# Third-layer units of a four-layer graph attention kernel: elementwise work from VectorE to GpSimd

## The chip, the core and the metric

The kernel runs on one core of one Trainium2 chip. The core has TensorE (PE), VectorE (DVE), ScalarE (ACT), GpSimd (POOL) and SyncE (SP), which work side by side, each through its own instructions in order. The metric is the device time of one execution in microseconds (us). Before the change the median of four runs is 1438.87 us (1433.23 to 1440.81).

## What is computed

Eight batches of 2048 nodes with 64 features pass through four layers over the same 2048x2048 0/1 matrix `adj`. Layers 0 to 2 are graph attention: every pair of nodes has a score, a softmax over the neighbours, and a weighted sum of features. Every layer ends with a residual and a layer normalization. Layer 3, the one that the change is about, has a softmax per feature:

```python
# after layer 2
x = _layernorm(x + _L2_gnn_ref(x, adj, ...), axis=-1)
# layer 3
feat = softplus(x * (INV_SQRT2 * w0) + b0)
scores = feat * wa + ba
attn = softmax(where(adj > 0, scores[j], -1e9), axis=j)   # per i and feature d
out = einsum('bijd,bjd->bid', attn, feat)
x = _layernorm(x + out, axis=-1)
```

Since the scores of layer 3 depend on j and d only, the kernel writes it as two products with the mask: numerator = mask @ (feat * exp(scores)), denominator = mask @ exp(scores), and divides.

## The kernel before

**Units.** `todo` lists 24 attention units (layer, batch): layers 0 and 1 in two halves of four batches, then layer 2 for batches 0 to 7. Below, (2,b) is the layer-2 unit of batch b. A unit runs over sixteen blocks jb of 128 neighbours. `weights` (line 920) makes a 128x2048 tile w on VectorE: the maximum of a row r and a column, times the mask. `exponential` (930) is done by ScalarE, and `products` (969) by TensorE, which sums four 512-wide products per block in PSUM. `reach` (949) emits the weights of layer 2 up to two blocks ahead of the products and the exponentials up to one ahead. The row r of layer 2 lies in PSUM; one buffer serves all units, and `spread` (767) has TensorE write the next unit's row over it once the last weights of a unit have read it.

**What runs beside a unit.** Python generators in `Streams` (1294) are stepped once per block (`bg.step()`), and every `yield` is a step. So the order of the instructions on each engine is written by the program, and the class `InOrder` (70) keeps it: every compute instruction goes through its line 80, which is why the profile gives nearly all of them as L80 and groups are told apart by the names of tiles.

**After a layer-2 unit** a chain of two generators runs during the next unit:
- `finish` (988): ScalarE copies the sums, TensorE transposes them (p_o), VectorE divides (den, o), adds the residual, and `stats` (508) gives sums, the sum of squares (sq_x) and, through GpSimd's power of -0.5 in `inv_std` (492, line 503), the two columns rs and nm. Line 506 has VectorE compute nm after the power. Then lines 1074 and 1075 normalize the rows: o * rs, and that + nm into x. The first needs only rs, the second nm too.
- `l3_features` (1109), one step later: SP stores x to HBM (1124), and `softplus` (381) follows: ScalarE's Abs and Exp, a step later Ln and Relu with two loads of its function table around them, a step later the sum f + y (389). In the step of that sum GpSimd computes the scores d in two instructions (1129, 1130) and VectorE reduces f over the nodes (fs, 1132). Two steps later ScalarE takes exp(d), one more step later comes the numerator f * d (1137).
- For the products both numerator and exponentials are split in two pieces: ScalarE copies the first (v, 1164), and the second is the difference (1168), four 128x512 instructions per batch. In the code before, the first batch of a pair (i = 0) has them on GpSimd and the second on VectorE. Batch 6 waits at line 1142 until the last unit is over.

**Layer 3's products** (`l3_products`, 1207) start when a pair of batches has both its pieces. TensorE multiplies 16x2 pieces with a block of the mask, half a block (16 products) per step, in between the attention products. The mask arrives in quarters by SP's queue (`fetch`, 1197, issued at 1202), five buffers ahead; after the last unit ScalarE and GpSimd make it by turns (`widen`, 1180). `l3_finish` (1259) then takes the reciprocal on VectorE, the product with the numerator, the residual and the second normalization on GpSimd while units still run, and the stores at line 1288.

**The phase.** `now[0]` is the layer of the running unit, 0 to 2, and becomes 3 at line 1424, when the loop over units is over and only the background streams go on. `l3_finish` already chooses its engine by it (`pool if now[0] < 3 else dve`, lines 1276 and 1284).

Of the kernel before, what the change touches and what calls it, by code (L numbers as in the profile page):

```python
# [15 lines left out]
ALU = mybir.AluOpType  # L16
# [34 lines left out]
def gnn4_kernel(ctx: ExitStack, tc: tile.TileContext, t, out):  # L51
# [55 lines left out]
    class Banks:  # L107
# [4 lines left out]
        pool = None  # L112
# [28 lines left out]
    pe, dve, act, pool = (InOrder(e) for e in (nc.tensor, nc.vector, nc.scalar, nc.gpsimd))  # L141
# [4 lines left out]
    def bc_f(v, n=K, f=F):  # L146
        return v[:, :, None].to_broadcast([P, n, f])

    def bc_k(v, n=K, f=F):
        return v[:, None, :].to_broadcast([P, n, f])  # L150
# [65 lines left out]
    src = t["L0_gnn_a"]  # L216
# [161 lines left out]
    nc.gpsimd.memset(ext[:, 1:2], -X_MAX)  # L378
    fext = consts.tile([P, 2], F32, name="fext")

    def softplus(f, y, src):

        act.activation(y, src, AF.Abs, scale=l3c[:, 0:1], bias=l3c[:, 1:2])
        act.activation(y, y, AF.Exp, scale=-1.0)
        yield 1
        act.activation(y, y, AF.Ln, bias=1.0)
        act.activation(f, src, AF.Relu, scale=l3c[:, 0:1], bias=l3c[:, 1:2])
        yield 1
        dve.tensor_tensor(f, f, y, ALU.add)

    rs_w, last_w, a_cols = [], [], [None]
    for layer in range(3):
        rs = early.tile([P, F1], F32, tag="rs_w", name=f"rs_{layer}")
# [594 lines left out]
    def finish(u):  # L988
        layer, b = u.layer, u.b
        yield from oT_slots.take()  # L990
        oT = tmp.tile([P, 2, 512], F32, tag="oT", name=f"oT_{u.n}")
        for c in range(2):
            act.copy(oT[:, c], u.acc[c])
        if layer == 0:
            hb = early.tile([P, K, F], F32, tag="hb", name=f"hb_{u.n}", bufs=1)
            for sl, y in V[0, b].parts:
                pool.tensor_tensor(
                    hb[:, :, sl], y, bc_k(gamma[:, sl], K, y.shape[2]), ALU.mult
                )
        yield 1  # L1000
        yield from o_slots.take()
        o = tmp.tile([P, K, F], F32, tag="o", name=f"o_{u.n}", bufs=2)
        o5 = o.rearrange("p (c h s) f -> p c s h f", c=2, h=2)
        done = 0
        while done < 4:
            width = Banks.width()
            ps = []
            yield from pm_slots.take(width)
            for i in range(done, min(done + width, 4)):
                c, s0 = i // 2, 2 * (i % 2)  # L1010
                p = psum(f"p_o_{u.n}_{c}_{s0}")
                for s in range(2):
                    k = s0 + s
                    pe.matmul(
                        p[:, s * 2 * F1 : (s + 1) * 2 * F1],
                        lhsT=oT[:, c, k * P : (k + 1) * P],
                        rhs=RH[layer].rearrange("p h f -> p (h f)"),
                        start=True,
                        stop=True,
                    )  # L1020
                ps.append((c, s0, p))
            done += width
            if done >= 4:
                oT_slots.give()
            yield 2 if width == 2 else 1
            for c, s0, p in ps:
                p4 = p[:, : 4 * F1].rearrange("p (s h f) -> p s h f", s=2, h=2)
                den = small.tile([P, 2, 2], F32, tag="den", name=f"den_{u.n}_{c}_{s0}")
                dve.reciprocal(den, p4[:, :, :, F])
                if layer == 2:  # L1030
                    dve.tensor_tensor(
                        o5[:, c, s0 : s0 + 2],
                        p4[:, :, :, :F],
                        den[:, :, :, None].to_broadcast([P, 2, 2, F]),
                        ALU.mult,
                    )
                    continue
                for s in range(2):
                    for h in range(2):
                        act.activation(  # L1040
                            o5[:, c, s0 + s, h],
                            p4[:, s, h, :F],
                            AF.Copy,
                            scale=den[:, s, h : h + 1],
                        )
            pm_slots.give(width)
        if layer == 2:
            for sl, x in x_cur[b].parts:
                dve.scalar_tensor_tensor(o[:, :, sl], o[:, :, sl], 0.0, x, ALU.max, ALU.add)
            yield 1  # L1050
        else:
            yield 1
            if layer == 0:
                pool.tensor_tensor(o, o, hb, ALU.add)
                yield 2

            yield from e_slots.take()
            e = tmp.tile([P, K, F], F32, tag="e", name=f"eh_{u.n}")
            act.activation(e, o, AF.Relu, scale=-1.0)
            act.activation(e, e, AF.Exp, scale=-1.0)  # L1060
            yield 1
            for sl, x in x_cur[b].parts:
                pool.tensor_tensor(
                    e[:, :, sl], e[:, :, sl], x, ALU.add
                )
            act.activation(o, o, AF.Relu)
            yield 1
            pool.tensor_tensor(o, o, e, ALU.add)
            e_slots.give()
            yield 2  # L1070
        nm, rs = yield from stats(o, K, f"x_{u.n}")
        xn = Rows(x_cur[b].t, layer < 2)
        if layer == 2:
            dve.tensor_tensor(o, o, bc_f(rs), ALU.mult)
            dve.tensor_tensor(xn.v, o, bc_f(nm), ALU.add)
        else:
            yield 1
            for k in range(K):
                act.activation(
                    xn.block(k), o[:, k], AF.Identity, scale=rs[:, k : k + 1], bias=nm[:, k : k + 1]  # L1080
                )
                if k % 4 == 3:
                    yield 1
            xn.settle()
        o_slots.give()
        x_cur[b] = xn
        V[layer + 1, b] = xn
        if layer < 2:
            yield 1
# [7 lines left out]
    now = [0, 0, 0]  # L1097
# [11 lines left out]
    def l3_features(b):  # L1109

        if b % 2 == 0:
            q = Pair()
            q.bs, q.n, q.fm, q.x, q.ready = [b, b + 1], f"{b}", {}, {}, 0
            pairs.append(q)
        else:
            q = pairs[-1]
        i = b % 2
        n = f"3_{b}"
        slots, tag = ((h_slots, "h"), (xT_slots, "xT"))[i]
        yield from slots.take()  # L1120
        yield from e_slots.take()
        f = x_cur[b].v
        q.x[i] = dram.tile([P, K, F], F32, tag="x3_d", name=f"x3_d_{b}", bufs=B)
        nc.sync.dma_start(q.x[i], f)
        y = tmp.tile([P, K, F], F32, tag="e", name=f"sp_{n}")
        yield from softplus(f, y, f)
        e_slots.give()
        d = tmp.tile([P, K, F], F32, tag=tag, name=f"d_{n}")
        pool.tensor_tensor(d, f, bc_k(wa), ALU.mult)
        pool.tensor_tensor(d, d, bc_k(l3off), ALU.add)  # L1130
        fs = small.tile([P, F], F32, tag="fs", name=f"fs_{n}")
        dve.tensor_reduce(fs, f.rearrange("p k f -> p f k"), AX.X, ALU.add)
        bg.add(l3_mean(q, i, fs, n))
        yield 2
        act.activation(d, d, AF.Exp)
        yield 1
        dve.tensor_tensor(f, f, d, ALU.mult)
        yield 1

        if i == 0:  # L1140
            if b == B - 2:
                while now[0] < 3:
                    yield 1
            else:
                yield from v_slots.take()
            q.v = [
                [
                    (work if b == B - 2 else late).tile(
                        [P, K2, 2, 2, F],
                        F32R,  # L1150
                        tag="w" if b == B - 2 else f"v{m}{h}",
                        name=f"v{m}_{h}_{q.n}",
                        bufs=4 if b == B - 2 else 1,
                    )
                    for h in range(2)
                ]
                for m in range(2)
            ]
        else:
            while not hasattr(q, "v"):  # L1160
                yield 1
        parts = [(h, w, (f, d)[w][:, h * K2 : (h + 1) * K2]) for h in range(2) for w in range(2)]
        for h, w, src in parts:
            act.copy(q.v[0][h][:, :, i, w], src)
        yield 1
        eng = dve if i else pool
        for h, w, src in parts:
            eng.tensor_tensor(
                q.v[1][h][:, :, i, w], src, q.v[0][h][:, :, i, w].bitcast(F32), ALU.subtract
            )  # L1170
        slots.give()
        yield 1
        q.ready += 1
# [759 lines left out]
```

## Time and profile before

| | |
|---|---|
| median of the runs | 1438.87 us |
| the profiled execution's own time | 1438.47 us |
| its span in the trace | 1436.7 us |
| last attention product (end of the units) | 1285.5 us |
| mean granted TensorE clock | 0.947 of full speed |

The span is what the trace covers, from the first instruction to the last; the execution's own time has 1.8 us around it. The page has the busy time of each engine, then the span in 40 equal slices of some 36 us whose digits are busy tenths. The layer-2 units take the 23rd to the 36th slice or so; what follows is layer 3 alone. Rows of an engine in order of time have start, duration, engine, operation and tiles, and in brackets the idle time before and what ended it.

### The profile page before, as it was taken

The page shows a single profiled execution, that of the slowest core. Times are in us where ns is not written, and L with a number is a line of the kernel's source. Part 1 is how long each engine was busy: PE and PEld are TensorE (multiplying, and loading weights), DVE is VectorE, ACT ScalarE, POOL GpSimd, SP SyncE. Part 2 cuts the span into 40 slices and gives each one's busy share as a digit, 9 for nine tenths or more (in the row PEclk, how much of TensorE's full clock was granted, in tenths as well). Part 3 has the DMA queues.
Part 4 walks back from the last instruction along what each step waited for, and adds up shares of the span by engine and source line. Part 5 has one row for each costly group of instructions (what it writes and reads, how often), then busy time and mean ns, then how long its engine had stood idle before and what let it go on. Part 6 is the DMA issues. An engine that isn't in the chain of part 4 may idle for free.

```text
span 1436.7 us, 19117 instructions
## 1 busy us (share of the span) xinstructions
PE 1235.9 (86%) x7138; PEld 620.6 (43%) x7138; DVE 1259.9 (88%) x1260; ACT 820.5 (57%) x1585; POOL 549.9 (38%) x619
## 2 busy tenths in 40 slices
PE   3679788988899988999998887879999898978896
PEld 2323233333233333344332332336565564648896
DVE  4699889997899999899999898898989989878876
ACT  4415444664557545555533986787677767574442
POOL 1152463324423344332322211312445535367665
PEclk9989999999999999999999897999999999999998
DMA  8730000000000022221201000005453354431111
GB/s 303 247 77 1 1 2 1 1 2 1 2 1 1 25 65 88 89 75 56 66 16 37 1 1 15 15 24 150 130 153 100 110 152 128 134 108 34 34 38 33
DMA packets 113335, 90.36 MB, mean 63 GB/s; under 512 B 58077, under 2 KB 91021, under 8 KB 112082
## 3 DMA queue, kind: packets, MB, share of 16 engines
q1 hardware_dynamic: 112690, 87.89, 20.4%
q8 instruction: 58, 0.95, 0.3%
q10 hardware_dynamic: 544, 1.17, 0.2%
q14 instruction: 43, 0.35, 0.1%
HBM read 63.54 MB, written 25.46 MB: 62 GB/s over the span
## 4 chain that ended last, share of the span: by engine, by line
PE 30%; DVE 19%; ACT 8%; issue 4%; POOL 2%; DMA 1%; SPq 0%; DVEq 0%; POOLq 0%; ACTq 0%
PE p_l L80 14%; PE acc L80 13%; DVE w L80 12%; ACT w L80 3%; DVE st_x L80 2%; ACT x L80 2%; PE p_o L80 1%; DVE o L80 1%; ACT sp L80 1%; DMA mask<-mask_d 1%; PE r L80 1%; POOL o L80 1%; DVE x L80 1%; DVE fs L80 1%; POOL st_x L80 1%
## 5 line engine op out<-in xcount | busy, mean ns | idle before, releaser
L80 DVE SCALAR_TENSOR_TENSOR w<-r,se,edge 128x2048 f32<-128x2048 f32 (+1 forms) x270 | 555.5, 2103 | 22.8 <-PE r L80 20.0
L80 PE MATMUL acc<-w,pv 128*64 128x512 f32 x2048 | 508.7, 629 | 71.0 <-DVE w L80 64.0
L80 DVE SCALAR_TENSOR_TENSOR w<-r,lo_g,edge 128x2048 f32<-128x2048 f32 (+1 forms) x144 | 298.0, 2096 | 18.0 <-PE r L80 9.7
L80 PE MATMUL acc<-w,x 128*64 128x512 f32 x1024 | 266.4, 651 | 38.6 <-ACT w L80 34.5
L80 ACT ACTIVATE w<-w,down_g 128x2048 f32<-128x2048 f32 (+1 forms) x144 | 257.4, 1809 | 70.5 <-DVE w L80 70.0
L80 PEld LDWEIGHTS p_l<-v,mask 128*128 128x128 f32 x2048 | 253.7, 194 | 66.1 <-issue 49.4
L80 PE MATMUL p_l<-v,mask 128*128 128x256 f32 x2048 | 269.7, 289 | 11.8 <-POOL mask L80 6.3
L80 PEld LDWEIGHTS acc<-w,pv 128*64 128x64 f32 x2048 | 133.3, 141 | 338.2 <-issue 190.4
L80 PEld LDWEIGHTS acc<-w,x 128*64 128x64 f32 x1024 | 67.8, 145 | 163.9 <-issue 91.4
L80 ACT COPY oT<-acc 128x512 f32<-128x512 f32 x48 | 25.8, 589 | 144.4 <-PE acc L80 144.4
L80 ACT ACTIVATE x<-o,st_x 128x64 f32<-128x64 f32 x256 | 90.6, 446 | 3.4 <-DVE st_x L80 3.4
L80 ACT ACTIVATE o<-p_o,den 128x64 f32<-128x64 f32 x256 | 55.9, 327 | 44.6 <-DVE den L80 44.6
L80 ACT ACTIVATE nd<-p_l,empty 128x256 f32<-128x256 f32 x64 | 30.2, 472 | 88.4 <-PE p_l L80 88.4
L80 POOL TENSOR_SCALAR isw_x<-isw_x 128x16 f32<-128x16 f32 x24 | 6.3, 262 | 181.3 <-DVE isw_x L80 169.8
L80 POOL TENSOR_TENSOR st_x<-isw_x,mhalf 128x16 f32<-128x16 f32 x24 | 70.4, 2931 | 2.0
L80 PEld LDWEIGHTS p_o<-rh,oT 128*128 128x128 f32 x384 | 49.7, 196 | 35.9 <-issue 15.4
L80 POOL TENSOR_TENSOR st_h<-isw_h,mhalf 128x16 f32<-128x16 f32 x8 | 23.6, 2953 | 106.4 <-DVE isw_h L80 83.5
L80 PE MATMUL p_o<-rh,oT 128*128 128x130 f32 x384 | 59.9, 293 | 4.6 <-ACT o L80 3.6
L80 DVE RECIPROCAL nd<-nd 128x256 f32<-128x256 f32 x32 | 55.8, 1743 | 0.0
L80 POOL TENSOR_TENSOR eh<-eh,x 128x1024 f32<-128x1024 f32 (+2 forms) x24 | 36.5, 1533 | 45.3 <-ACT eh L80 45.2
L80 POOL COPY x<-x 128x16 f32<-128x16 f32 x16 | 3.3, 206 | 123.8 <-ACT x L80 123.8
L80 DVE SCALAR_TENSOR_TENSOR w<-row,se,edge 128x2048 f32<-128x2048 f32 x16 | 39.6, 2485 | 10.0 <-DMA row<-row_d 10.0
(243 smaller groups left out, 1486.5 us busy)
## 6 DMA issues: line engine op xcount, KB each, us to landing
mask<-mask_d SPq DMA_DIRECT2D x140, 256.0 KB
mask_d<-mf SPq DMA_DIRECT2D x32, 512.0 KB
raw<-in_adjT_dram SPq DMA_DIRECT2D x8, 1024.0 KB
raw<-in_adjT_dram SPq DMA_DIRECT2D x16, 512.0 KB
x<-in_x_dram SPq DMA_DIRECT2D x8, 512.0 KB
x_d<-x SPq DMA_DIRECT2D x8, 512.0 KB
e<-x_d SPq DMA_DIRECT2D x64, 64.0 KB
out_dram<-o SPq DMA_DIRECT2D x64, 64.0 KB
```

Source lines behind the costliest of these rows:

```text
L80: ins = f(*args, **kwargs)
```

## The change

Four places take their engine from the phase: normalization of layer 2, sum of softplus, numerator, and second pieces run on GpSimd while units run and on VectorE after. The engine of the second pieces no longer depends on the place i of the batch in its pair. The call of softplus for two constants at the start keeps VectorE. No instruction is added or left out, and no `yield` moves.

```diff
-    def softplus(f, y, src):
+    def softplus(f, y, src, eng=dve):
...
-        dve.tensor_tensor(f, f, y, ALU.add)
+        eng.tensor_tensor(f, f, y, ALU.add)
...
         if layer == 2:
-            dve.tensor_tensor(o, o, bc_f(rs), ALU.mult)
-            dve.tensor_tensor(xn.v, o, bc_f(nm), ALU.add)
+            side = pool if now[0] < 3 else dve
+            side.tensor_tensor(o, o, bc_f(rs), ALU.mult)
+            side.tensor_tensor(xn.v, o, bc_f(nm), ALU.add)
...
-        yield from softplus(f, y, f)
+        side = pool if now[0] < 3 else dve
+        yield from softplus(f, y, f, side)
...
-        dve.tensor_tensor(f, f, d, ALU.mult)
+        side = pool if now[0] < 3 else dve
+        side.tensor_tensor(f, f, d, ALU.mult)
...
-        eng = dve if i else pool
+        eng = pool if now[0] < 3 else dve
         for h, w, src in parts:
             eng.tensor_tensor(
                 q.v[1][h][:, :, i, w], src, q.v[0][h][:, :, i, w].bitcast(F32), ALU.subtract
             )
```

## The prediction

> **What bounds the kernel now.** I read the page first, then the table by stretch with one row per attention unit of layer 2, then the chain of waits, then each engine in order of time where a moved instruction stands. I write (2,b) for the time in which batch b's unit ends on TensorE; the third-layer work of batch b-1 runs beside it.
>
> ```profile
> PE 1235.9 (86%) x7138; PEld 620.6 (43%) x7138; DVE 1259.9 (88%) x1260; ACT 820.5 (57%) x1585; POOL 549.9 (38%) x619
> ...
> PE   3679788988899988999998887879999898978896
> ...
> DVE  4699889997899999899999898898989989878876
> ACT  4415444664557545555533986787677767574442
> POOL 1152463324423344332322211312445535367665
> ```
>
> VectorE has the largest share (88%), GpSimd the smallest (38%), so the page suggests a gain. But the share is an average; the units are what counts:
>
> ```profile
> core 0: us, PE busy (x) PEld busy (x) DVE busy (x) ACT busy (x) POOL busy (x), PEclk, DMA share, GB/s
> ...
> 835.70:896.30 60.60, 47.62 (x249) 17.62 (x250) 54.66 (x65) 46.32 (x46) 8.44 (x7) 0.83 0.02 9
> 896.30:951.50 55.20, 43.89 (x351) 16.92 (x347) 48.20 (x44) 44.16 (x34) 16.50 (x13) 0.88 0.04 14
> 951.50:1012.80 61.30, 58.76 (x346) 33.91 (x346) 56.17 (x51) 45.28 (x37) 14.90 (x17) 1.00 0.38 114
> 1012.80:1079.00 66.20, 64.78 (x396) 39.57 (x393) 58.76 (x61) 46.15 (x40) 28.02 (x35) 1.00 0.51 143
> 1079.00:1147.90 68.90, 61.08 (x354) 34.83 (x350) 63.95 (x69) 49.06 (x45) 36.52 (x43) 0.98 0.35 100
> 1147.90:1217.00 69.10, 64.50 (x379) 38.36 (x378) 62.92 (x63) 46.86 (x39) 29.87 (x37) 0.98 0.47 141
> 1217.00:1285.50 68.50, 62.25 (x363) 36.10 (x359) 56.70 (x61) 46.33 (x43) 31.69 (x39) 0.95 0.40 118
> ```
>
> In (2,1) and (2,2) TensorE idles 24.3 us and VectorE leads. From (2,3) on the third layer's products stand between the attention products and TensorE is almost full: 22.6 us idle in 334 us. A faster VectorE can take no more than these 47 us, and in the last five units only where TensorE waits for it. After 1285.5 the code keeps VectorE.
>
> **What moves.** The condition is read when an instruction is emitted, so I count by place. Normalization: seven batches, two instructions each (batch 7's follow the last unit). Sum of softplus: seven. Numerator: six; batch 6's (at 1287.95) follows the exponential that ScalarE does after the last unit's first copies, at least one step later, so it stays. Second pieces: batches 1, 3, 5 (four each) go to GpSimd, and batch 6's four go the other way, because they are always emitted after the last unit.
>
> ```profile
> L80 DVE TENSOR_TENSOR x<-o,st_x 128x1024 f32<-128x1024 f32 x8 | 11.2, 1404 | 0.3
> L80 DVE TENSOR_TENSOR x<-x,sp 128x1024 f32<-128x1024 f32 x8 | 9.8, 1225 | 11.4 <-ACT x L80 11.4
> L80 DVE TENSOR_TENSOR x<-x,d 128x1024 f32<-128x1024 f32 x8 | 9.7, 1217 | 5.3 <-ACT d L80 5.3
> ```
>
> ```profile
> L80 POOL TENSOR_TENSOR d<-d,l3off 128x1024 f32<-128x1024 f32 x8 | 19.2, 2405 | 0.6
> ```
>
> VectorE loses 7 x (1.21 + 1.40) + 7 x 1.23 + 6 x 1.22 + 12.8 (the twelve pieces, contended ones included) - 4 x 0.68 = 44 us of work. GpSimd's row for the same shape is 2.40 us (2.38 to 2.44 undisturbed) and its pieces take 1.28, so it gains 27 x 2.40 + 12 x 1.28 - 4 x 1.28 = 75 us; at 28 to 37 of 69 us per unit it has room. The price is latency: +2.4 us for a normalization, +1.2 for a sum.
>
> **The wait that is added.** Behind the softplus sum VectorE has nothing but the reduction of its result, in the same step:
>
> ```profile
> 1196.28 1.23 DVE L80 TENSOR_TENSOR x<-x,sp 128x1024 f32<-128x1024 f32 x1 [1.07 <-ACT x L80]
> 1197.55 2.05 DVE L80 TENSOR_REDUCE fs<-x 128x64 f32<-128x1024 f32 x1
> 1199.51 2.35 DVE L80 SCALAR_TENSOR_TENSOR w<-r,lo_g,edge 128x2048 f32<-128x2048 f32 x1
> 1201.76 0.74 DVE L80 SCALAR_TENSOR_TENSOR st<-st 128x4 f32<-128x4 f32 x1
> ```
>
> VectorE is in order and already waited 1.07 us for ScalarE here. Now it waits 2.40 us instead of working 1.23, so its queue moves back by 1.2, not forward. Queued behind are the weights w. And ScalarE's Abs, at the head of the softplus, waits for the slower normalization; Exp, Ln, Relu and the exponentials of w queue behind it. Who waits for that is in TensorE's order: the row r of the next unit overwrites what the last weights read.
>
> ```profile
> 1206.52 1.28 PE L80 MATMUL r<-row,ones 3*128 3x512 bf16 x4 [4.11 <-DVE w L80]
> ```
>
> **Unit by unit**, by the starts in the rows:
> - (2,1): GpSimd's power ends at 860.55 and the first half of the normalization needs only that; VectorE's small st_x instruction is held until it ends (863.2), the second half ends at 865.8. Abs starts there instead of 864.57; Relu ends 1.2 later, the sum 2.4 instead of 1.2 after it. The 2.4 us that VectorE wins before turn into idle. The row r, for which TensorE stood 3.54 us, comes later: +1.8 us.
> - (2,2): GpSimd must first finish its amT pieces (to about 927.3 without contention), the normalization ends at 932.2, Abs 3.0 late, reduction 4.2 late, r 4.2 late. Numerator (1.1) and pieces (2.4) leave VectorE afterwards, but ScalarE's copies follow TensorE's end, so they pay back 0.6: +3.6 us.
> - (2,3): sum behind the last weights, TensorE full: 0. (2,4): same; the product o<-nd no longer collides with the normalization, TensorE's 0.75 us wait for the mask behind it in SP's queue goes: -0.7.
> - (2,5): the pieces held VectorE 4.58 us. TensorE's waits from 1112 to 1141 (0.81, 0.85, 1.80, 1.56, 0.71, sum 5.7) partly go; GpSimd needs 8 x 1.28 = 10.2 us, ready for the first product at 1112.49. Small two-input instructions now wait for it, ScalarE's table loads stay: between -1.6 and -3.4, I take -2.5.
> - (2,6): GpSimd reaches the normalization at 1185.2 (behind o<-o,e), ends at 1190.0; Abs 2.5 late, the reduction 3.6 late, r at 1210.2: +3.7.
> - (2,7): ScalarE's casts bound it; sum behind the last weights: 0.
> - Tail: the sum on GpSimd delays its out rows by 1.1, SP's queue holds mask fetches behind their transfers, TensorE waits for those at 1292.57: +1.1. Batch 6's pieces (2.7 us) fit into VectorE's 3.5 us idle before 1296.6; without that cover they cost up to 2.7.
>
> TensorE works at half pace after long waits (3.68 us for eight products at 940.26, 1.94 at 933.45). Longer waits in (2,2) and (2,6) may cost 0 to 1.8 each; I take 1.0, between the ends: +2.0.
>
> Sum: 1.8 + 3.6 - 0.7 - 2.5 + 3.7 + 1.1 + 2.0 = +9.0 on the profiled execution's 1438.5: **1447.5**. That execution is 0.4 under the median of the runs.
>
> **Contention.** A VectorE instruction with two SBUF inputs is held by GpSimd: beside its pieces the 128x512 subtraction took 1.78 us against 0.68 alone, and the st row above 0.74 against 0.15, ending with GpSimd's d. The weights read r from PSUM, and d beside them stays at 2.38 to 2.44. So I price moved work beside w at nothing, and the small instructions at 0 to 2.3 us each.
>
> [...]
>
> **Rivals.**
> - **Relief counts** (faster): if the run-ahead of two weights covers the new waits, VectorE's chain gives back 3.6 in (2,1), 7.3 in (2,2) and 4.6 in (2,5): 1438.5 - 15.5 = 1423; partly, to 1431. For: VectorE is the chain from 853 to 883. Against: sum and reduction are adjacent, so there is no run-ahead between them. It decides if r comes no later than now in (2,1), (2,2) and (2,6).
> - **Wash** (same): waits as forecast, but without the clock terms and with (2,5) giving its whole 5.7: +3.8, about 1442.
> - **The lock spreads** (much slower): two more small VectorE instructions per unit held by 2.4 us in VectorE-led places, five units: 5 x 2.4 = 12 more, 1459.
>
> That the change does less than it says is in the count: one batch of eight stays, one runs the other way.
>
> **Numbers.** Forecast 0.44, wash 0.29, relief 0.15, lock 0.12. A run tells no less than 0.5% (7.2 us) from no change: faster is under 1431.7, slower over 1446.1. About a tenth of the forecast's chance lies under 1446.1, a little of the wash under 1431.7: slower 0.52, same 0.32, faster 0.16. The likeliest case alone spans 1443 to 1453; the range goes on to part of the relief, 1427, and to the lock, 1461.
>
> **What would show it.** VectorE's busy time falls by about 44 us and GpSimd's rises by 75. The reduction fs stands behind GpSimd's x with some 2.4 us more idle in each of seven units. TensorE's wait before r grows in (2,1), (2,2), (2,6); its waits around 1115 to 1135 shrink. I am wrong if r is not later there, if GpSimd's 128x1024 instructions take far from 2.4 us, or if mask waits of several us appear.

## The result and the profile after

The changed kernel takes 1441.58 us (median of 44 runs), the kernel before 1438.17 (70 runs): ratio 1.0027, 95% interval [1.0018, 1.0036], some 3.9 us of 1438. (Medians are of all runs; the ratios, here and below, are of undisturbed runs, and ratios are compared in place of medians.) It is slower, by less than the 0.5% that the chances were set against. The forecast of 1447.5 had the sign and was 6 us too high: +9.0 was forecast, more than twice what came. The profiled execution took 1444.21 us, its span is 1442.4.

The page after, busy time by engine:

```profile
PE 1230.9 (85%) x7138; PEld 619.6 (43%) x7138; DVE 1225.7 (85%) x1225; ACT 820.2 (57%) x1585; POOL 607.0 (42%) x654
```

VectorE lost 34 us (forecast 44) and GpSimd gained 57 (forecast 75). By the sum of durations the moved instructions took 43.2 us off VectorE, as worked out, but its other instructions grew by 6.5: the small isw rows by 3.9, o<-o,x by 1.5, held by GpSimd (the page counts records that overlap once, hence 34). On GpSimd the moved work adds 67.5, while what was there before got some 10 us shorter (o<-nd 0.87 to 0.73 us each, o<-o,e 0.91 to 0.73). The groups of GpSimd by shape give the price of each moved instruction (busy us, mean ns):

```profile
L80 POOL TENSOR_TENSOR x<-x,sp 128x1024 f32<-128x1024 f32 x7 | 16.6, 2374 | 49.5 <-ACT x L80 49.5
...
L80 POOL TENSOR_TENSOR x<-x,d 128x1024 f32<-128x1024 f32 x6 | 14.3, 2382 | 6.4 <-ACT d L80 6.4
L80 POOL TENSOR_TENSOR x<-o,st_x 128x1024 f32<-128x1024 f32 x7 | 13.3, 1903 | 0.7 <-DVE st_x L80 0.2
```

Sum and numerator take the 2.4 us that they were priced at, the normalization takes 1.90 for each of its two instructions. The counts are as worked out: seven sums, seven normalizations, six numerators.

The table by stretch after, with the columns of the prediction's (busy time of PE, PEld, DVE, ACT, POOL, then granted clock), for (2,2) and (2,6):

```profile
897.20:957.20 60.00, 44.19 (x347) 16.79 (x347) 45.10 (x41) 44.11 (x34) 23.04 (x17) 0.91 0.04 13
...
1151.00:1222.50 71.50, 64.97 (x383) 38.46 (x379) 58.99 (x58) 46.73 (x39) 39.68 (x44) 0.95 0.46 134
```

VectorE is busy for 3.1 us less in (2,2) and for 3.9 less in (2,6), and both are longer. The next two fences show why: VectorE in order of time, then ScalarE, around the softplus.

```profile
942.21 1.98 DVE L80 TENSOR_REDUCE fs<-x 128x64 f32<-128x1024 f32 x1 [7.95 <-POOL x L80]
...
1202.48 1.98 DVE L80 TENSOR_REDUCE fs<-x 128x64 f32<-128x1024 f32 x1 [5.29 <-POOL x L80]
```

```profile
932.04 1.24 ACT L80 ACTIVATE sp<-x,l3c 128x1024 f32<-128x1024 f32 x1 [2.55 <-POOL x L80]
```

The reduction fs now waits for GpSimd's x in all seven units (3.1 to 8.0 us each), and ScalarE's Abs waits for GpSimd's normalization (in (2,2) 2.55 us, before 0.52). Units on TensorE, measured from end to end (us; in brackets, when the row r started after the unit's start), and the tail, from the last unit's end to the end of the span. An end is taken here at the start of a unit's last small products, 0.4 us before they are over:

| | (2,1) | (2,2) | (2,3) | (2,4) | (2,5) | (2,6) | (2,7) | tail |
|---|---|---|---|---|---|---|---|---|
| before | 60.62 (47.9) | 55.16 (48.9) | 61.35 | 66.24 | 68.83 (57.1) | 69.18 (59.0) | 68.41 | 151.6 |
| after | 59.47 (48.5) | 59.99 (52.1) | 60.85 | 65.23 | 67.75 (55.2) | 71.51 (60.8) | 67.85 | 152.4 |
| after - before | -1.15 | +4.83 | -0.50 | -1.01 | -1.08 | +2.33 | -0.56 | +0.8 |

The sum is +3.7, near the timed +3.9; both columns are single executions, and some of their numbers move by as much between executions of one kernel (below). The spans differ by 5.7; the other 2.0 arise before (2,1) starts, where no instruction differs. In the sixteen profiles of this study that start lies between 830.7 and 839.6 us. So spans are not compared below; units are, and ratios over many runs.

TensorE around the row of (2,2), before and after:

```profile
944.82 1.02 PE L80 MATMUL r<-row,ones 3*128 3x512 bf16 x4 [0.32 <-DVE w L80]
945.77 5.37 PE L80 MATMUL acc<-w,x 128*64 128x512 f32 x24
```

```profile
948.88 1.02 PE L80 MATMUL r<-row,ones 3*128 3x512 bf16 x4 [1.86 <-DVE w L80]
949.83 7.02 PE L80 MATMUL acc<-w,x 128*64 128x512 f32 x24
```

The row comes 3.2 us later, counted from the unit's start, and the same 24 products behind it take 7.0 in place of 5.4 us: TensorE is partly at half pace, its granted clock 0.50 from 949.8 to 953.1, 0.98 from there to 957.0. (In (2,1), at 0.50, eight such products take 3.68 us, at 1.00 they take 1.94.) Both parts of +4.83 are in these two lines.

### The profile page after: what moved, and what is told of

Same layout as the page of the kernel before. It is cut to its first block, busy times and chain, and to the rows that moved or that the text cites. A ratio compares the mean times of both kernels' runs of the same rounds, so it can differ in the third digit from the quotient of the medians.

```text
span 1442.4 us, 19115 instructions
## 1 busy us (share of the span) xinstructions
PE 1230.9 (85%) x7138; PEld 619.6 (43%) x7138; DVE 1225.7 (85%) x1225; ACT 820.2 (57%) x1585; POOL 607.0 (42%) x654
## 4 chain that ended last, share of the span: by engine, by line
PE 30%; DVE 17%; ACT 10%; issue 4%; POOL 3%; DMA 1%; POOLq 0%; DVEq 0%; SPq 0%; ACTq 0%
PE acc L80 13%; PE p_l L80 13%; DVE w L80 11%; ACT w L80 3%; DVE st_x L80 2%; ACT x L80 2%; ACT sp L80 2%; PE p_o L80 1%; POOL x L80 1%; DVE o L80 1%; PE r L80 1%; DVE nd L80 1%; ACT L80 1%; ACT v L80 1%; POOL st_x L80 1%
## 5 line engine op out<-in xcount | busy, mean ns | idle before, releaser
L80 DVE SCALAR_TENSOR_TENSOR w<-r,lo_g,edge 128x2048 f32<-128x2048 f32 (+1 forms) x144 | 298.0, 2096 | 22.1 <-PE acc L80 10.9
L80 PE MATMUL acc<-w,x 128*64 128x512 f32 x1024 | 263.4, 644 | 41.0 <-ACT w L80 37.0
L80 PEld LDWEIGHTS p_o<-rh,oT 128*128 128x128 f32 x384 | 50.1, 197 | 36.4 <-issue 15.4
L80 PE MATMUL r<-row,ones 3*128 3x512 bf16 x92 | 26.1, 406 | 29.0 <-DVE w L80 27.9
```

The source lines that it names most:

```text
L80: ins = f(*args, **kwargs)
```

## The experiments

Three theories run through them. **Chain**: what is lost is the longer way from normalization to softplus sum to row r. **Lock**, or holding: VectorE's instructions with two SBUF inputs are held while GpSimd works (in the kernel before a 128x512 subtraction beside GpSimd's pieces took 1.78 us, alone 0.68). **Clock**: TensorE's pace after its waits (in the kernel before eight products took 3.68 us behind a wait of 4.88, 1.94 behind one of 1.29). Each kernel was timed against the kernel before on the same chip; the groups e1 to e4, e5 to e10, e11 to e14 and e15 with e16 were on four chips. Ratios have 95% intervals, and "us" is the ratio's distance from 1 times 1438.

| run | what GpSimd has, or what else differs | median | ratio | us |
|---|---|---|---|---|
| e3_num_pieces | numerator and pieces alone | 1436.55 | 0.9994 [0.9978, 1.0009] | -0.9 |
| e9_norm_only | normalization alone | 1441.05 | 1.0010 [0.9987, 1.0034] | +1.4 |
| e5_sum_only | softplus sum alone | 1449.48 | 1.0065 [1.0034, 1.0096] | +9.3 |
| e1_sum_back | all but the sum | 1436.25 | 0.9991 [0.9972, 1.0011] | -1.3 |
| e2_norm_back | all but the normalization | 1448.28 | 1.0069 [1.0047, 1.0091] | +9.9 |
| after | all | 1441.58 | 1.0027 [1.0018, 1.0036] | +3.9 |
| e7_sum_twice | all, the sum done twice | 1458.94 | 1.0154 [1.0126, 1.0181] | +22.1 |
| e4_fs_later | all, fs two steps later | 1439.92 | 1.0019 [1.0002, 1.0037] | +2.7 |
| e14_beside_sum | as e3, an idle addition beside the sum | 1441.21 | 1.0029 [1.0009, 1.0049] | +4.2 |
| e10_filler | all, TensorE's waits half filled | 1440.43 | 1.0021 [0.9996, 1.0046] | +3.0 |
| e13_after_more_filler | all, waits filled in three units | 1435.03 | 0.9990 [0.9972, 1.0007] | -1.4 |
| e12_before_filler | nothing, filled in two units | 1431.35 | 0.9975 [0.9958, 0.9992] | -3.6 |
| e16_before_filler3 | nothing, filled in three units | 1433.35 | 0.9961 [0.9943, 0.9980] | -5.6 |
| e11_pieces_filler | as e3, filled in two units | 1429.42 | 0.9956 [0.9938, 0.9974] | -6.3 |
| e15_pieces_filler3 | as e3, filled in three units | 1427.30 | 0.9932 [0.9911, 0.9954] | -9.8 |

The units that the text below uses, from the profiled executions:

| | (2,1) | (2,2) | (2,5) | (2,6) | seven units | tail |
|---|---|---|---|---|---|---|
| before | 60.62 (47.9) | 55.16 (48.9) | 68.83 (57.1) | 69.18 (59.0) | 449.8 | 151.6 |
| after | 59.47 (48.5) | 59.99 (52.1) | 67.75 (55.2) | 71.51 (60.8) | 452.7 | 152.4 |
| e3_num_pieces | 60.61 (47.9) | 55.18 (48.9) | 68.38 (55.9) | 70.15 (58.7) | 449.4 | 148.8 |
| e1_sum_back | 61.45 (47.4) | 60.64 (50.9) | 67.31 (54.7) | 71.37 (59.5) | 454.7 | 149.2 |
| e2_norm_back | 63.57 (50.8) | 59.19 (50.1) | 68.95 (56.4) | 73.02 (62.0) | 460.0 | 151.2 |
| e5_sum_only | 63.57 (50.8) | 59.20 (50.1) | 71.70 (57.6) | 74.10 (63.2) | 463.6 | 150.0 |
| e9_norm_only | 61.37 (47.4) | 60.75 (51.0) | 69.95 (55.9) | 70.29 (59.5) | 456.3 | 149.9 |
| e7_sum_twice | 63.69 (50.9) | 63.09 (54.5) | 71.70 (57.6) | 73.85 (63.2) | 466.7 | 154.4 |
| e4_fs_later | 60.48 (47.6) | 59.47 (50.0) | 68.61 (54.9) | 65.90 (55.1) | 442.7 | 161.5 |
| e14_beside_sum | 60.33 (49.4) | 59.24 (49.6) | 67.60 (55.9) | 74.85 (63.0) | 456.5 | 150.0 |
| e10_filler | 61.28 (48.5) | 58.38 (52.1) | 69.31 (55.2) | 72.78 (60.7) | 455.7 | 149.7 |
| e12_before_filler | 56.26 (47.9) | 58.87 (48.9) | 69.62 (57.1) | 66.83 (58.3) | 446.6 | 149.2 |
| e11_pieces_filler | 56.24 (47.9) | 58.91 (48.9) | 67.61 (55.9) | 68.43 (59.9) | 446.0 | 148.7 |
| e16_before_filler3 | 56.24 (47.9) | 55.21 (49.0) | 69.70 (57.1) | 68.58 (58.4) | 445.8 | 149.4 |
| e13_after_more_filler | 56.87 (48.5) | 58.37 (52.1) | 67.77 (55.2) | 69.19 (60.7) | 446.2 | 150.0 |
| e15_pieces_filler3 | 56.24 (47.9) | 55.21 (49.0) | 67.61 (55.9) | 68.13 (59.6) | 442.2 | 149.0 |

### Which part costs what

**e1_sum_back**: the sum goes back to VectorE.

```diff
-        yield from softplus(f, y, f, side)
+        yield from softplus(f, y, f)
```

> The changed kernel with the sum of softplus back on VectorE; normalization, numerator and second pieces stay on GpSimd. In the trace of the changed kernel the rows r of (2,1), (2,2) and (2,6) come 0.6, 3.2 and 2.4 us late. Chain theory: the sum on GpSimd (2.34 to 2.41 us against 1.23) accounts for 1.1 of each, since the reduction fs and the last weights queue behind it; without it the loss of 3.4 us shrinks by 3.3, to about the time before (-1.0 to +1.5). Lock theory (VectorE's small two-input instructions held by GpSimd): the loss goes with GpSimd's added time, of which the seven sums are a quarter, so +2.6. Clock theory (TensorE's pace in (2,1) and (2,2) by accident): no order, and VectorE's idle time ahead of fs does not matter.

Measured -1.3 us [-4.0, +1.6]: as the chain theory had it, and against the lock theory's +2.6. The interval of the changed kernel lies above 1, so the sum on GpSimd is what makes it slower. In the traces the row r is 1.2, 1.2 and 1.3 us later in (2,1), (2,2) and (2,6) with the sum on GpSimd (after against e1), the 1.1 each of the chain. The units of e1's single profile don't show the gain: together with the tail they take 2.6 us more than before, where the timed runs have -1.3. (2,2) alone has 5.5 more, with r 2.0 later and TensorE at half pace in the two blocks ahead of r (3.68 us each) and partly behind it (7.99 us for the 24 products, before 5.37).

**e2_norm_back**: the normalization goes back to VectorE.

```diff
-            side = pool if now[0] < 3 else dve
-            side.tensor_tensor(o, o, bc_f(rs), ALU.mult)
-            side.tensor_tensor(xn.v, o, bc_f(nm), ALU.add)
+            dve.tensor_tensor(o, o, bc_f(rs), ALU.mult)
+            dve.tensor_tensor(xn.v, o, bc_f(nm), ALU.add)
```

> The changed kernel with the normalization of layer 2 back on VectorE; sum, numerator and pieces stay on GpSimd. Chain theory: Abs starts in time again, so r is late by the sum alone: +1.1 in each of three units in place of 0.6, 3.2, 2.4; that is 2.8 less than the changed kernel, +0.6 against before. Lock theory: the normalization is 40% of GpSimd's added time, so +2.0, and VectorE's busy time grows by 18 us.

Measured +9.9 us: both theories missed. Leaving one costly part out made the kernel slower. The next runs came from this.

**e3_num_pieces**: both edits above; only numerator and second pieces stay on GpSimd.

> Only the numerator and the second pieces move to GpSimd; normalization and sum stay on VectorE. Chain theory: r is in time everywhere and what remains are the gains of (2,2) to (2,5): -2 against before (-4 to 0). Lock theory: GpSimd's pieces hold VectorE in (2,5), o<-o,x 2.8 us in place of 1.3: +1.

Measured -0.9 [-3.2, +1.3], not clear of zero, and neither the chain's -2 nor the lock's +1 is ruled out. The rows r of (2,1), (2,2) and (2,6) are where they were before, to 0.3 us.

**e5_sum_only**: the kernel before with the sum alone moved (the diff's `eng` argument and the `side` of softplus, nothing else).

> The kernel before with the softplus sum alone on GpSimd (normalization, numerator and second pieces stay as they were). Chain theory by itself: the reduction and the row r 1.15 later in (2,1), (2,2) and (2,6), and nothing else: +3.5 us, about 1441.8. Chain with holding (what the kernel with the normalization back on VectorE suggested, where the sum cost 11.7 us): beside the 1.15 each, VectorE's small group instructions in (2,1) are held 2.4 us while the sum runs, and the end of layer 3 comes about 2.4 later: +7 to +12, about 1447. Lock theory, in proportion to GpSimd's added time (16 of 57 us): +1, about 1439.3.

Measured +9.3: chain with holding, nearly three times the chain's own +3.5. In the trace, VectorE in (2,1) before, then with the sum moved, then GpSimd in the same stretch:

```profile
872.55 0.34 DVE L80 TENSOR_SCALAR sc_g<-sc_g 128x4 f32<-128x4 f32 x2
872.93 0.16 DVE L80 SCALAR_TENSOR_TENSOR sc_g<-lim_g,sc_g 128x4 f32<-128x4 f32 x1
```

```profile
868.89 2.43 DVE L80 TENSOR_SCALAR sc_g<-sc_g 128x4 f32<-128x4 f32 x2
871.35 2.21 DVE L80 SCALAR_TENSOR_TENSOR sc_g<-lim_g,sc_g 128x4 f32<-128x4 f32 x1
873.49 1.92 DVE L80 TENSOR_REDUCE fs<-x 128x64 f32<-128x1024 f32 x1
```

```profile
868.75 2.34 POOL L80 TENSOR_TENSOR x<-x,sp 128x1024 f32<-128x1024 f32 x1 [11.69 <-ACT x L80]
871.17 2.37 POOL L80 TENSOR_TENSOR d<-x,wa_bc 128x1024 f32<-128x1024 f32 x1
```

These instructions work on four elements a partition. The first row is two of them: one took 2.22 us, until GpSimd's sum was over, the other its usual 0.17. The SCALAR_TENSOR_TENSOR ends 0.02 us after GpSimd's d. So two small instructions are held, for 4.1 us together, and because fs stands behind them, r comes 2.9 us later in (2,1), not 1.15. In the changed kernel VectorE is done with them at 873.83, 0.7 us before the sum starts at 874.54: the normalization is off VectorE, so it arrives earlier. The sum costs 10.8 us without the moved normalization (e2 against e3) and 5.2 with it (after against e1). The holding explains part of that: r of (2,1) is 2.9 later in the one pair and 1.2 in the other. The rest was not taken apart. Two parts of one change are not additive.

**e9_norm_only**: the kernel before with the normalization alone moved.

> The kernel before with the normalization alone on GpSimd. Chain theory: ScalarE's Abs 2.0 later in (2,2) and 1.6 later in (2,6), not later in (2,1), and the row r with it: +2 to +4, about 1441. If the normalization costs as little as between the kernel with only the sum back and the one with only numerator and pieces on GpSimd: 0, about 1438. Lock theory, in proportion to GpSimd's time (27 of 57 us): +1.6.

Measured +1.4 [-1.9, +4.9]: it does not tell 0 from +2. In the trace r is 2.1 later in (2,2), as the chain had it, but only 0.5 later in (2,6), not 1.6, and 0.6 earlier in (2,1).

**e7_sum_twice**: GpSimd does the sum twice, first into the tile d.

```diff
+        if twice is not None and eng is pool:
+            eng.tensor_tensor(twice, f, y, ALU.add)
         eng.tensor_tensor(f, f, y, ALU.add)
```

> The changed kernel with GpSimd doing each softplus sum twice while units run, the first time into the tile that the scores d overwrite next (extra work that the layer does not need). Chain theory: the reduction and the row r come 2.35 us later in (2,1), (2,2) and (2,6): +7 over the changed kernel, about 1448.5; with a longer half-pace of TensorE after the longer waits up to 1452. Lock theory, in proportion to GpSimd's added time (16.5 us on 57 us that cost 3.4): +1, about 1442.5. If VectorE's stand behind the sum were hidden: 0.

Measured +22.1 against before, 18.2 over the changed kernel: more than twice the chain's +7, and 18 times the lock theory's +1. Row r is 2.4 later in four units, not three, since (2,5) follows too: 9.6. The units are 4.2, 3.1, 4.0 and 2.3 longer, 13.6 in all, and the tail 2.0. The direction and the size per row are the chain's; what the chain lacks is what stands behind r. Pace is part of it: behind r in (2,1) two blocks took 3.68 us, in the changed kernel one, and the mean granted clock of these six executions was 0.941, of the kernel before beside them 0.945. The trace accounts for 16.0 from the start of (2,1), the timed runs for 18.2.

**e4_fs_later**: fs and its mean are issued two steps later, behind the last weights.

```diff
-        dve.tensor_reduce(fs, f.rearrange("p k f -> p f k"), AX.X, ALU.add)
-        bg.add(l3_mean(q, i, fs, n))
         yield 2
+        dve.tensor_reduce(fs, f.rearrange("p k f -> p f k"), AX.X, ALU.add)
+        bg.add(l3_mean(q, i, fs, n))
```

> The changed kernel, all four parts on GpSimd, with the reduction fs and the mean that follows it two steps later, behind the last weights of the unit. Chain theory: nothing stands between ScalarE's late Relu and the last weights any more, so r comes earlier by the idle time ahead of fs and by fs itself in (2,1), (2,2) and (2,6), up to what ScalarE's table loads allow: 2 to 4 us at each place, in all -6 against the changed kernel, -3 against before (-9 to -1). Lock theory: the same instructions meet the same GpSimd work, +3.4 stays. Clock theory: +3.4 within 2.

Measured +2.7: the total missed. r came without a wait in (2,2) and (2,6), as meant, but (2,2) still took 59.47, and the 5.6 and 5.7 us won in (2,6) and (2,7) came back as 9.1 in the tail: Abs of batch 5 starts 55.6 us into (2,6) where it started 41 us in after the change, and work was pushed behind the last unit. That the later mean holds its PSUM buffer longer and so shifts the streams is my guess; it was not tried by itself.

### Holding, by itself

**e14_beside_sum**: e3 with an addition on GpSimd that nothing reads, beside VectorE's sum.

```diff
+        if beside is not None and now[0] < 3:
+            pool.tensor_tensor(beside, y, y, ALU.add)
         eng.tensor_tensor(f, f, y, ALU.add)
```

> Only numerator and second pieces on GpSimd, the softplus sum on VectorE, and beside it an addition of the same size on GpSimd (y + y into the tile that the scores overwrite next; nothing reads it and VectorE's sum doesn't wait for it). Holding theory: it starts with the end of Ln, and the two-input instructions of VectorE that meet it wait for its end: the small group instructions in (2,1) by about 2, the sum itself by 1 in the other units, r later by that: +3 to +8 against 1436.5, about 1442. Latency theory (only what waits for GpSimd's result is late): the scores d come 1 to 2 later, nothing else: 0 to +1.

Measured +4.2 against before, 5.0 over e3. VectorE in (2,1) and (2,2):

```profile
866.98 1.58 DVE L80 TENSOR_TENSOR sc_g<-lim_g 128x4 f32<-128x4 f32 x1
...
932.01 1.89 DVE L80 TENSOR_TENSOR x<-x,sp 128x1024 f32<-128x1024 f32 x1 [1.05 <-ACT x L80]
```

Before, the first took 0.16 and the second 1.22. Nothing waits for the addition's result, so the added 1.4 and 0.7 us are holding, and r is later by the same 1.5 and 0.7. That it costs time by itself is shown; the size of 5.0 is not holding alone, because in (2,6) TensorE also waited 2.05 us for a mask, which e5 and e2 had too (2.05 and 2.34) and the changed kernel had not. Why the mask was late there was not tried.

### TensorE's pace

**e10_filler**: products of a constant by itself in TensorE's waits; the place is called behind Relu, behind the sum and behind p_fm.

```diff
+    def filler(place):
+        if now[1] in fills:
+            n = fills[now[1]][place]
...
+            for _ in range(n):
+                pe.matmul(p[:, :P], lhsT=ones, rhs=ones, start=True, stop=True)
```

> The changed kernel with products of a constant by itself (128x128, into a PSUM buffer that nothing reads) put into TensorE's waits of (2,1) and (2,2) behind the softplus: 20 in (2,1), 26 in (2,2), each some 0.35 us at full pace, so that they fill most of each wait and delay nothing by design. Clock theory: TensorE is no longer idle for long and keeps full pace: eight products of a block take 1.9 and not 3.5 to 3.7 us on both sides of the row r; the row itself still waits for the last weights, so the gain is what stood behind it, 1.7 in (2,1) and 1.65 in (2,2): -3.4 against the changed kernel, about 1438. Chain theory alone: what follows the row waits for VectorE and ScalarE anyway: 0, about 1441.5; and a loss of up to 2 if the filling ends after the wait.

Measured +3.0, 0.9 under the changed kernel, inside the intervals. The trace is clear in (2,2):

```profile
947.13 1.02 PE L80 MATMUL r<-row,ones 3*128 3x512 bf16 x4 [1.85 <-DVE w L80]
948.08 5.37 PE L80 MATMUL acc<-w,x 128*64 128x512 f32 x24
```

r starts as late as after the change (52.1), and the products behind it are back at 5.37: 59.99 became 58.38, -1.6 as expected. A product took about 0.24 us, not the expected 0.35, so the waits were half filled: in (2,1) a wait of 3.45 us before r was left, the two blocks behind r stayed at 3.68 us, and nothing was won there. The next runs filled more.

**e12_before_filler**, **e11_pieces_filler**, **e13_after_more_filler**: the numbers of products per place (behind Relu, sum, p_fm) in units 17, 18 and 22 of `todo`, which are (2,1), (2,2) and (2,6); the last of them go into p_fm's own buffer.

```diff
+    fills = {17: (0, 14, 20), 22: (0, 0, 14)}                      # e11, e12
+    fills = {17: (0, 14, 22), 18: (18, 16, 12), 22: (0, 0, 20)}    # e13
```

> The kernel before with the same filling (34 products in (2,1), 14 in (2,6)), nothing moved to GpSimd. Clock theory: -3 to -6 against before, about 1434, as much as the filling gives to the kernel with only numerator and pieces moved. Chain theory: 0.

> Only numerator and second pieces on GpSimd (as in the kernel that was 1.7 us under before), and TensorE's waits filled with products of a constant by itself that nothing reads: 34 in (2,1), all behind the softplus and before the row r, and 14 before r in (2,6). Clock theory: in (2,1) the three blocks behind r run at full pace, start to start 2.8 and not 4.55 us, as far as the weights keep up: -2 to -4; in (2,6) r takes 1.0 and not 1.86 and the next block 1.9 and not 3.7: -1 to -2. Together about 1433, and this one beats both kernels. Chain theory alone: the weights behind r set the pace anyway: 0, about 1436.5.

> The changed kernel with the waits of (2,1), (2,2) and (2,6) filled nearly whole (36, 46 and 20 products). Clock theory: r and the blocks behind it at full pace in all three: (2,2) 58.4 as with the smaller filling, (2,1) 57 to 59 in place of 59.5 to 61.3, (2,6) 69 to 70 in place of 71.5 to 72.8: -3 to -6 against the changed kernel, about 1437, that is the level of before. The row r itself stays as late as in the changed kernel (48.5, 52.1 and 60.8 after the unit's start): what is left against before with the same filling, 3 to 4 us, is then the chain's. Chain theory alone: 0.

Measured -3.6, -6.3 and -1.4: each 5 us under the same kernel without filling, except e12 with 3.6. First a block of products behind r in (2,1) of the kernel before, then the same kernel filled (e12), in (2,1) and in (2,2), where e12 does not fill:

```profile
884.98 3.68 PE L80 MATMUL acc<-w,x 128*64 128x512 f32 x8
```

```profile
881.66 1.02 PE L80 MATMUL r<-row,ones 3*128 3x512 bf16 x4 [0.70 <-DVE w L80]
882.61 1.94 PE L80 MATMUL acc<-w,x 128*64 128x512 f32 x8
...
938.92 1.86 PE L80 MATMUL r<-row,ones 3*128 3x512 bf16 x4 [0.27 <-DVE w L80]
940.71 8.23 PE L80 MATMUL acc<-w,x 128*64 128x512 f32 x24
```

In (2,1) r took 1.86 and the blocks 3.68 each unfilled; filled, 1.02 and 1.94, and the unit is 4.4 us shorter with r at the same 47.9. In (2,2) r also comes at the same time as before (48.9), but this time TensorE was at half pace: 8.23 in place of 5.37, and the unit 58.87 in place of 55.16. So an r at 48.9 does not settle what (2,2) takes: in the first profile the granted clock was 0.60 from 944.0 to 944.4 and 1.00 from there on, that is back some 0.5 us before r; by the pace of the products it came back at most 0.3 us before r in e3 (55.18; p_fm 0.69 us, r 1.02, the 24 products 5.37) and, as I estimate from 8.23 and 8.28 us for the 24, some 7.6 us after r's start in e12 and e11 (58.9). Both of the latter fill (2,1) and both of the former don't, so whether chance or that filling decides it is not shown.

**e15_pieces_filler3** and **e16_before_filler3**: (2,2) filled as well.

```diff
+    fills = {17: (0, 14, 20), 18: (10, 17, 7), 22: (0, 0, 14)}
```

> Only numerator and second pieces on GpSimd, with TensorE's waits filled in (2,1) (34 products), (2,2) (34) and (2,6) (14). With the filling in (2,1) and (2,6) alone, (2,2) took 58.9 us though its row r came at the same 48.9 as in the kernel before, where it took 55.2: the blocks behind r ran at half pace. Clock theory: filled, (2,2) takes 55.2 again: -3.7 on the 1430.7 of that kernel, about 1427, 0.7% under before. If the 58.9 had another cause: 0, about 1430.7.

> The kernel before with its waits filled in (2,1), (2,2) and (2,6) (34, 34 and 14 products), nothing moved. Clock theory: (2,1) 56.2, (2,2) 55.2, (2,6) 67 to 69: -3.7 on the 1433.4 of the kernel with two of the three filled, about 1430. This is the kernel to hold the changed kernel with all three filled against (1435.6): what is left then, about 5.5 us, is what the change costs where TensorE keeps its pace, by later rows r ((2,2) +3.2, (2,1) +0.6, (2,6) +1.8 to 2.4) less what it wins elsewhere. Without the clock theory, this kernel stays at 1433.4 and the difference at 2.

Measured -9.8 and -5.6. (2,2) takes 55.21 in both; in e15:

```profile
938.87 1.02 PE L80 MATMUL r<-row,ones 3*128 3x512 bf16 x4 [0.67 <-DVE w L80]
939.82 5.37 PE L80 MATMUL acc<-w,x 128*64 128x512 f32 x24
```

e15 beats both kernels: its interval ends at 0.9954, the changed kernel's begins at 1.0018. And e16 beside e13 shows the change with the three units filled: 4.2 us dearer by the ratios (each known to about 2.6, so +0.5 to +8). In the profiles the pace behind r is the same in (2,1) and (2,2) (1.94 us a block, 5.37 for the 24 products), but not in (2,6), where the 16 products behind r took 3.65 us in e13 and 5.35 in e16. The traces of the two differ by less, 596.1 against 595.2 us from the start of (2,1) on: +0.6, +3.2 and +0.6 in (2,1), (2,2) and (2,6), -1.9 in (2,5), -2.1 in the three full units ((2,3), (2,4), (2,7)), +0.6 in the tail. The expected 5.5 is inside the timed interval, the traces speak for less. Whether it is nearer 1 or 5 stays open, and the two kernels were timed on different chips.

## Why the prediction was right and wrong

The mechanism was right: the sum's latency stands between VectorE's weights and the row r (e1, e7), and the relief of VectorE does not pay for it. Two terms of the sum were mis-sized, and both pushed the forecast up.

- **The normalization's price** was the failed step. I priced it at "GpSimd's row for the same shape is 2.40 us". The shape was the same, the second operand was not: in that row (d<-d,l3off) it is a row of 64 repeated for every node, in the normalization a column repeated along the features. The kernel before had that very form, in its groups of GpSimd:

```profile
L80 POOL TENSOR_TENSOR pv<-y,se 128x1024 f32<-128x1024 f32 x8 | 15.2, 1903 | 0.0
```

  1.90 for 2.40, twice per batch, is 1.0 us per unit: the normalization came to 3.80 on GpSimd against 2.61 on VectorE, 1.2 more and not the 2.4 that I wrote (my own rows gave 2.2). So Abs was 0.14, 2.03 and 0.94 late in (2,1), (2,2), (2,6), where I had 1.2, 3.0 and 2.5, and r 0.6, 3.2 and 1.8 late, where I had 1.8, 4.2 and 3.7. Some 3 us of the 6 too many are this. In (2,6) another 0.65 is contention that went away: I put GpSimd's o<-o,e, ahead of the normalization, at its 1.84 us of before, when VectorE's normalization ran beside it; it took 0.73, and GpSimd reached the normalization 37.05 us into the unit, where VectorE had started it at 37.06.
- **(2,1)**: forecast +1.8, measured -1.15 (r +0.62). TensorE returned to full pace one block earlier after the change than before (one block at 3.68 us behind r, before two). I take this for accident: in e10, with r at the same 48.5, it returned one block later and the unit took 61.28. With the pace held (e13 against e16) the unit is +0.63, as r is.
- **(2,2)**: forecast +3.6 and 1.0 for the clock, measured +4.83: 3.2 by the row, 1.65 by the pace. The clock term was inside its bounds of 0 to 1.8.
- **(2,6)**: forecast +3.7 and 1.0, measured +2.33; with the waits filled (e13 against e16) +0.6, though r is 2.3 later there: the 16 products behind r took 3.65 us in the one and 5.35 in the other, which is the 1.7 between.
- **The clock term** (+2.0) was the second mis-sized one. I let the change add half pace in two units; but the kernel before pays it too, 4.4 us in (2,1), and in these two profiles the pace fell for the change there (-1.8) and against it in (2,2) (+1.65). The net of these two is about nothing, and so it is over many executions: the mean granted clock was 0.949 in 44 of the changed kernel and 0.947 in 100 of the kernel before.
- **(2,3), (2,4), (2,7)**: 0, -0.7 and 0 forecast; -0.5, -1.0 and -0.6 measured. **Tail**: +1.1 forecast, +0.8 measured; but the kernel before has 151.6, 149.2 and 149.4 in three executions (before, e12, e16), so this +0.8 says little.
- **(2,5)**: -2.5 forecast, -1.08 measured, short of the bound of -1.6. The row r did come 1.95 earlier, but TensorE's waits, which the term was made of, did not shrink: the 1.80 went, others grew, and 1.11, 0.85, 2.24 and 1.59 make 5.8 in place of 5.7. TensorE's busy time fell by 1.6 instead, at a granted clock of 1.00 for 0.98. GpSimd's pieces held VectorE's small instructions: o<-o,x 2.80 for 1.30, two isw rows 0.98 and 1.21 for 0.15 each. I had named this and charged too little; how much of the missing gain it is was not tried.
- **Contention**: "the small instructions at 0 to 2.3 us each" held: 0.4 to 1.4 more each in the changed kernel's units, 2.1 in e5. Not only instructions with two SBUF inputs are held: the TENSOR_SCALAR of e5 has one (2.22 us for 0.17). The holding that I gave 0.12 as a rival (its 5 x 2.4 counts one hold per unit, though it names two) is real, and e5 and e2 pay it; the changed kernel escapes it in (2,1) by 0.7 us. I did not see that the moved normalization is what lets it escape.
- **Relief counts** failed where it was said to be decided: r is later in (2,1), (2,2) and (2,6). **Wash**, +3.8 without the clock terms, came closest in the sum, 1442 against 1441.58, though not by its reason: (2,5) did not give its whole 5.7.
- What would show it: fs behind GpSimd's x in seven units, r later in three, both seen (r in (2,5) came earlier). VectorE's 34 and GpSimd's 57 were less than the 44 and 75, and GpSimd's normalization was away from 2.4. TensorE's waits near 1115 to 1135 did not shrink in sum. Mask waits of several us did not come; in the tail there were two, of 1.3 and 1.0 us (before 0.2 and 1.2).

How TensorE's pace went with its waits differs between executions. Behind a wait of 2.85 us a block of eight products took 1.94 in one (e12) and 2.79 in another (e3), behind 4.88 us 3.68 (the kernel before, e11, e12); where 3.45 us of a wait were left unfilled (e10), the two blocks behind it stayed at 3.68. In (2,1) of the kernel before TensorE worked for 9.9 us from r on, almost without a gap, before the clock came back (granted clock 0.50 from 882.9 to 893.1, 1.00 behind it), after the change for 5.9. So the half pace that I gave to the change alone belongs to both kernels, and how long it lasts differs from execution to execution; what sets its start and its end is not shown.

## What to carry to other kernels

Price a moved instruction by a row with the same operands, not only the same shape: on GpSimd a 128x1024 instruction took 1.90 us here with a repeated column, 2.34 to 2.41 with two full tiles, 2.39 with a repeated row. Before moving work off a busy engine, look at what stands next in that engine's queue: numerator and pieces have nobody right behind them and went without a loss that shows (-0.9 us, interval -3.2 to +1.3), a sum whose reduction is the next instruction turned 1.23 us of work into 2.34 to 2.41 of waiting, and on the other engine it and the scores behind it held what else was in the queue (in e5 two small instructions, 2.22 and 2.21 us for 0.17 and 0.16). Where TensorE waits for several us, the units of one profile mix a change under 1% with TensorE's pace (here (2,2) took 55.16 and 58.87 with r at the same 48.9): fill the wait with idle products and compare again, and keep the filling if it pays, as it did here for all three kernels that had two or three units filled.

## What the runs showed of the hardware

- GpSimd's elementwise instruction on 128x1024 took 2.34 to 2.41 us with two full operands (x<-x,sp and x<-x,d after the change), on average 2.39 and 2.40 with a row repeated for every node (d<-x,wa_bc and d<-d,l3off), 1.90 with a column repeated along the row (x<-o,st_x), and 1.89 with the same tile twice (d<-sp in e14).
- Two instructions of VectorE on 128x4 elements, one of them a TENSOR_SCALAR with a single input, were held for 2.1 us each by GpSimd's 128x1024 instructions (e5): two of those followed each other at 868.75 and 871.17, and the small instruction behind the first, at 871.35, met the second.
- Idle products on a constant did not delay r where they fit into a wait (47.9 with and without; a product is two records of 0.12 us, 40 of them took 4.68 us before r in e16) and gave 4.4 us in (2,1) of the kernel before.
- The same instructions up to the start of (2,1) took 830.7 to 839.6 us in sixteen profiled executions: that scatter of 8.9 us is larger than this change (3.9).
